# A four-level attention stack on one core: level 0's self attention as thirteen written steps, and level 2's steps reordered

## The chip, the cores and the metric

The kernel runs on one core of a Trainium2 chip. The metric is device time in microseconds (us) from launch to end; the median of three runs of the kernel before is 4409.24 us (4403.62 to 4411.94). The engines are named as the profile names them: PE (TensorE; its weight loads are PEld), DVE (VectorE), ACT (ScalarE), POOL (GpSimd) and SP (SyncE, which here only issues transfers).

## What is computed

A residual stream x of 64 sequences, 32 tokens and 256 features (2048 rows) goes through four levels of three layers: cross attention with a context, self attention, and a feed-forward layer, each on the layer norm of x and added to x. Two of the twelve layers matter here. Level 0's self attention has 16 heads of 16 features, with a root-mean-square norm of each head's query and key:

```python
def rms_norm(x, w):
    ms = jnp.mean(x * x, axis=-1, keepdims=True)
    return x * jax.lax.rsqrt(ms + EPS) * w
q = rms_norm(proj(Wq), qn_w)
k = rms_norm(proj(Wk), kn_w)
v = proj(Wv)
scores = jnp.einsum('bhnd,bhmd->bhnm', q, k) * scale
attn = jax.nn.softmax(scores, axis=-1)
out = jnp.einsum('bhnm,bhmd->bhnd', attn, v)
return out.transpose(0, 2, 1, 3).reshape(B, N, D) @ Wo.T
```

Level 2's self attention has 16 heads of 64 features, unit-length queries and keys, two constant extra keys a head, and a distance bias on the scores. Attention stays within one sequence of 32 tokens in both.

## The kernel before

The rows lie in 16 tiles of 128 rows (four sequences each), which stay in on-chip memory in self.x. Every layer is a loop over the 16 tiles (NT). All matrix work is float32 on PE; the results land in PSUM[...].

Level 0 self attention (`l0_attn`, L762 to L849) is a generator `body(i)` with four yields. `skewed` advances all live bodies once per round, oldest first, so five tiles are in flight: in one round tile i-4 makes its block diagonal of probabilities, its weighted sum of values and its output; i-3 its scores and softmax; i-2 its unit-length queries and keys (`qk`, L797, on POOL) and their transposes; i-1 its projections (queries and keys `pqk`, values `pv`), squares (L788) and mean squares (L792, L793) and the power -1/2 of these (`qk_r`, in `rsqrt`, L391 to L393, on POOL); tile i its layer norm (`layer_input`). Scores are 64 small matmuls (32 by 32 by 64); `kb` holds each key head pair twice, with one head of the pair zeroed by the weight kw, made by DVE at L804. `diagonal` (L872) is four DVE transposes of 32 by 512. PSUM is split into three banks "m" (projections, transposes, output), four for the scores "s", and one "o" for the weighted sum.

Level 2 self attention (`l2_attn`) has the same work as named steps, and a list written out by hand that says which step of which tile comes in which order within a round (i, i-1, i-2 and the next tile's norm i+1). `lengths(t, k)` sums the squares (L1928), bounds them (L1929) and takes the power on POOL (L1931), `unit` multiplies (L2041), `scores` ends with the maximum (L2083), the subtraction (L2084) and the exponential (L2085), `output` adds into x (L2120).

What sets the order on an engine: each engine runs its own stream in order and waits on semaphores. The streams are made by the tile framework, which schedules instructions as it believes that their operands and buffers become ready and takes the order in the program as a preference among those that are ready. So the streams need not follow the text, and in the trace they don't everywhere: in level 2 the maximum L2083 is written before the second half's multiply L2041, and runs behind it. All matmuls through the helper `mm` are recorded at L438, transposes at L432 (`transposed`) or L2151 (`transposed_into`).

Of the kernel before, what the change touches and what calls it, by code (L numbers as in the profile page):

```python
# [28 lines left out]
NB = 4  # L29
# [289 lines left out]
class Perceiver:  # L319
# [442 lines left out]
    def l0_attn(self):  # L762
# [3 lines left out]
        with ExitStack() as st:  # L766
            one = st.enter_context(tc.tile_pool(name="l0a_1", bufs=1))
            pool = st.enter_context(tc.tile_pool(name="l0a", bufs=3))
            ps = st.enter_context(tc.tile_pool(name="l0a_p", bufs=3, space=PSUM))
            bds = self.zeroed(one, [128, 16, NB, T], "bd")  # L770

            vs = self.zeroed(one, [128, 16, 32], "v", 4)
            qw = self.sb(one, [128, 1], "qw")
            nc.vector.tensor_scalar(qw, self.col("L0_attn_qn_w"), 0.25, None, ALU.mult)
            kw = self.sb(one, [128, 2], "kw")
            nc.vector.tensor_scalar(kw, self.table("pair"), self.col("L0_attn_kn_w"), None, ALU.mult)

            def body(i):
                _, nT = self.layer_input(pool, ps, i, "m")
                yield  # L780
                pqk = self.sb(ps, [128, 32, 16], "m")
                self.mm(pqk.rearrange("p h d -> p (h d)"), [(nT[:, k, :], wqkv[:, k, 0:512]) for k in range(2)])
                pv = self.sb(ps, [128, 16, 16], "m")
                self.mm(pv.rearrange("p h d -> p (h d)"), [(nT[:, k, :], wqkv[:, k, 512:768]) for k in range(2)])
                v = vs[i % 4]
                nc.scalar.copy(v[:, :, 0:16], pv)
                sq = self.sb(pool, [128, 32, 16], "sq")
                nc.scalar.activation(sq, pqk, AF.Square)  # L788
                raw = self.sb(pool, [128, 32, 16], "raw")
                nc.scalar.copy(raw, pqk)  # L790
                ms = self.sb(pool, [128, 32], "ms")
                nc.vector.tensor_reduce(ms, sq, AX.X, ALU.add)  # L792
                nc.vector.tensor_scalar(ms, ms, 1.0 / 16, None, ALU.mult)  # L793
                r = self.rsqrt(pool, ms, float(np.finfo(np.float32).eps), "qk_r")
                yield
                qk = self.sb(pool, [128, 32, 16], "qk")
                nc.gpsimd.tensor_tensor(qk, raw, bcast(r, 2, 16), ALU.mult)  # L797
                pT = self.transposed(ps, qk.rearrange("p h d -> p (h d)"), "m", 4)
                qT = self.sb(pool, [128, 2, 128], "qT")
                nc.scalar.activation(qT, pT[:, 0:2, :], AF.Copy, scale=qw)  # L800

                kb = self.sb(pool, [128, 2, NB, 2, T], "kb")
                for c in range(2):
                    nc.vector.tensor_tensor(  # L804
                        kb[:, c],
                        bcast(pT[:, 2 + c, :].rearrange("p (b t) -> p b t", b=NB), 2, 2),
                        bcast(bcast(kw, 1, NB), 3, T),
                        ALU.mult,
                    )
                yield  # L810

                psc = self.sb(ps, [128, 4, 512], "s", bufs=1)
                for c in range(2):
                    for r in range(4):
                        for b in range(NB):
                            q = slice(b * T, (b + 1) * T)
                            f = slice(32 * r, 32 * r + 32)
                            self.mm(
                                psc[q, r, c * 64 : c * 64 + 64],
                                [(qT[f, c, q], kb[f, c, b].rearrange("p h t -> p (h t)"))],  # L820
                            )
                sv = psc[:, :, 0:128].rearrange("p r (c h k) -> p c r h k", c=2, h=2)
                e = self.sb(pool, [128, 16, T], "hs_e")
                mx = self.sb(pool, [128, 16], "hs_m")
                for c in range(2):
                    ev = e[:, 8 * c : 8 * c + 8, :].rearrange("p (r h) k -> p r h k", r=4)
                    mv = mx[:, 8 * c : 8 * c + 8].rearrange("p (r h) -> p r h", r=4)
                    nc.vector.tensor_reduce(mv, sv[:, c], AX.X, ALU.max)
                    nc.vector.tensor_tensor(ev, sv[:, c], bcast(mv, 3, T), ALU.subtract)
                nc.scalar.activation(e, e, AF.Exp)  # L830
                rs = self.softmax_heads(pool, e, 16, T)
                p = self.sb(pool, [128, 16, T], "hs_p")
                nc.gpsimd.tensor_tensor(p, e, bcast(rs, 2, T), ALU.mult)
                yield
                bd = bds[i % 2]
                self.diagonal(bd, p)
                po = self.sb(ps, [128, 4, 128], "o", bufs=1)
                for h in range(16):
                    self.mm(
                        po[32 * (h % 4) : 32 * (h % 4) + 32, h // 4, :],  # L840
                        [(v[:, h, :], bd[:, h].rearrange("p b t -> p (b t)"))],
                    )
                oT = self.sb(pool, [128, 4, 128], "oT")
                nc.scalar.copy(oT, po)  # L844
                py = self.sb(ps, [128, D], "m")
                self.mm(py, [(oT[:, k, :], wo[:, k, :]) for k in range(4)])
                nc.vector.tensor_tensor(self.x[:, i, :], self.x[:, i, :], py, ALU.add)

            skewed(body(i) for i in range(NT))  # L849

    def heads_softmax(self, pool, src, bd, scale, plus=0.0):

# [1059 lines left out]
    def l2_attn(self):  # L1912
# [3 lines left out]
        with ExitStack() as st:  # L1916
# [148 lines left out]
            def scores(i):  # L2065
# [9 lines left out]
                for hh in range(2):  # L2075
# [3 lines left out]
                        bias.rearrange("p (c a) k -> p a c k", a=2)[:, hh],  # L2079
                        ALU.add,  # L2080
                    )
                mx = self.sb(pool, [128, 16], "mx")
                nc.vector.tensor_reduce(mx, s, AX.X, ALU.max)  # L2083
                nc.vector.tensor_tensor(s, s, bcast(mx, 2, K), ALU.subtract)  # L2084
                nc.scalar.activation(s, s, AF.Exp)  # L2085
                t_p[i] = s

            def divided(i):
                s = t_p[i]
# [33 lines left out]
            norm_1(0), norm_2(0), norm_3(0), turned(0)  # L2123
            for i in range(NT + 2):
                steps = [
                    (i, lambda t: projected(t, 0)),
                    (i, lambda t: lengths(t, 0)),
                    (i + 1, norm_1),
                    (i - 2, weighted),
                    (i, lambda t: projected(t, 1)),  # L2130
                    (i, lambda t: unit(t, 0)),
                    (i, lambda t: lengths(t, 1)),
                    (i + 1, norm_2),
                    (i - 1, scores),
                    (i - 2, output),
                    (i, lambda t: unit(t, 1)),
                    (i - 1, divided),
                    (i + 1, norm_3),
                    (i, value_rows),
                    (i, lambda t: heads_first(t, 0)),  # L2140
                    (i + 1, turned),
                    (i - 1, diagonal),
                    (i, lambda t: heads_first(t, 1)),
                ]
                for t, step in steps:
# [292 lines left out]
```

## Time and profile before

| | us |
|---|---|
| median of 3 runs | 4409.24 |
| profiled execution, own time | 4408.68 |
| its span, first to last instruction | 4406.9 |
| level 0 self attention, first square to last add into x | 399.12 to 632.07 |
| level 2 self attention, first square to last copy of a weighted sum | 2418.7 to 2820.6 |

| whole span | PE | PE weight loads | DVE | ACT | POOL |
|---|---|---|---|---|---|
| busy us | 3820.6 | 2664.1 | 1896.2 | 1177.4 | 1181.6 |
| share | 87% | 60% | 43% | 27% | 27% |

How to read the lines of the profile: `L792 DVE TENSOR_REDUCE ms<-sq 128x32 f32<-128x512 f32` is line 792 of the kernel, its engine, its operation, the tile written and the tiles read (buffer numbers left out) and their shapes. In a timeline the first number is the start in us from the start of the span, the second the duration, and a bracket gives how long the engine was idle before it and what released it. In a table of windows, "busy (x)" is an engine's busy time and number of instructions in that stretch, and PEclk is the TensorE clock that was granted, as a share of full speed. In a list of waits, the numbers are the total us, how many times, and the longest. A whole-span share is a mean over stages with different limits.

### The profile page before, as it was taken

How to read it: one execution, taken by the hardware profiler on the slowest of the kernel's cores; microseconds unless marked ns; L12 is line 12 of the kernel's file. 1: busy time of each engine (PE TensorE's matmuls, PEld its weight loads, DVE VectorE, ACT ScalarE, POOL GpSimd, SP SyncE). 2: the span in 40 equal slices, each digit the busy share in tenths (PEclk: the TensorE clock that was granted, in tenths of full speed). 3: DMA queues.
4: the chain of work that ended last, by engine and by line, in shares of the span. 5: the costliest groups of instructions: out<-in, count | busy, mean ns of one | idle time of the engine just before them, and what ended most of it. 6: DMA issues, size and time to landing. Idle time of an engine off the chain costs nothing.

```text
span 4406.9 us, 68988 instructions
## 1 busy us (share of the span) xinstructions
PE 3820.6 (87%) x27148; PEld 2664.1 (60%) x27148; DVE 1896.2 (43%) x5310; ACT 1177.4 (27%) x3159; POOL 1181.6 (27%) x1638
## 2 busy tenths in 40 slices
PE   7997662879898596989998888899999999999996
PEld 6785441556676364767675555444444677777774
DVE  5554654244444605565655555301000344444335
ACT  2342220123332022333332333201111233333331
POOL 5434641033311135444443333100000211112102
PEclk9998875989999698999999899999999999999997
DMA  6351021175000143222221000200001111110000
GB/s 213 123 160 37 1 108 65 42 234 166 3 2 28 55 124 109 73 71 69 79 73 51 1 1 1 81 0 0 0 0 38 37 33 33 33 33 21 2 2 22
DMA packets 162996, 245.25 MB, mean 56 GB/s; under 512 B 27521, under 2 KB 105745, under 8 KB 158449
## 3 DMA queue, kind: packets, MB, share of 16 engines
q1 hardware_dynamic: 152370, 224.92, 16.4%
q0 software_dynamic: 5280, 10.82, 1.1%
q10 hardware_dynamic: 5024, 5.11, 0.3%
q8 instruction: 215, 3.52, 0.3%
q14 instruction: 107, 0.88, 0.1%
HBM read 223.80 MB, written 16.99 MB: 55 GB/s over the span
## 4 chain that ended last, share of the span: by engine, by line
PE 43%; DVE 8%; POOL 6%; ACT 3%; issue 2%; DMA 1%; DVEq 0%; ACTq 0%; POOLq 0%; SPq 0%
PE m L438 20%; PE h L438 13%; PE s L438 4%; POOL sr L1931 2%; PE b L438 1%; PE e L2327 1%; ACT e L2314 1%; DVE t L2342 1%; POOL p L1874 1%; PE m L1880 1%; POOL cT L1835 1%; DVE qn L2041 1%; DVE ss L1928 1%; PE o L438 1%; PE m L432 1%
## 5 line engine op out<-in xcount | busy, mean ns | idle before, releaser
L438 PE MATMUL m<-w,oT 128*128 128x256 f32 x1344 | 336.9, 403 | 21.7 <-ACT oT L844 9.8
L438 PEld LDWEIGHTS m<-w,oT 128*128 128x128 f32 x1344 | 265.8, 201 | 78.5 <-ACT oT L844 14.0
L438 PE MATMUL m<-nTg,w 128*128 128x256 f32 x1024 | 231.3, 385 | 1.3 <-ACT nTg L1323 1.1
L438 PE MATMUL h<-h,w 128*128 128x512 f32 x512 | 220.4, 592 | 0.0
L438 PE MATMUL h<-h,h 128*128 128x512 f32 x512 | 220.4, 592 | 0.0
L2203 DVE TENSOR_TENSOR y<-m,row_L_ffn_w_s 128x256 f32<-128x256 f32 x16 | 6.8, 425 | 486.6 <-PE m L438 486.6
L438 PEld LDWEIGHTS m<-nTg,w 128*128 128x128 f32 x1024 | 193.5, 191 | 28.9 <-ACT nTg L1323 1.7
L2314 ACT ACTIVATE e<-s,nm 128x257 f32<-128x257 f32 x256 | 118.2, 474 | 321.6 <-DVE nm L2313 263.2
L438 PE MATMUL m<-w,nT 128*128 128x512 f32 (+2 forms) x384 | 173.9, 595 | 30.2 <-DVE x L2120 28.9
L438 PE MATMUL s<-cT,ut 128*128 128x257 f32 x768 | 186.0, 388 | 3.7 <-ACT p L1870 2.9
L438 PE MATMUL m<-pT,cn 128*128 128x384 f32 x512 | 177.3, 489 | 0.0
L1874 POOL TENSOR_TENSOR p<-p,rs 128x771 f32<-128x771 f32 x64 | 94.9, 1483 | 298.9 <-DVE rs L1873 260.7
L438 PEld LDWEIGHTS h<-h,w 128*128 128x128 f32 x512 | 97.3, 190 | 122.5 <-issue 122.5
L438 PEld LDWEIGHTS h<-h,h 128*128 128x128 f32 x512 | 97.3, 190 | 122.5 <-issue 122.5
L2204 POOL TENSOR_TENSOR x<-x,y 128x256 f32<-128x256 f32 x16 | 11.9, 744 | 591.8 <-DVE y L2203 591.8
L438 PEld LDWEIGHTS m<-v,eT 128*128 128x128 f32 x1280 | 158.5, 192 | 9.0 <-ACT qT L695 1.8
L872 DVE STREAM_TRANSPOSE bd<-hs_p 32x512 f32<-32x512 f32 x192 | 134.9, 702 | 59.5 <-POOL hs_p L866 38.7
L438 PEld LDWEIGHTS s<-cT,ut 128*128 128x128 f32 x768 | 143.9, 195 | 27.0 <-issue 4.2
L438 PE MATMUL m<-v,eT 128*128 128x64 f32 x1280 | 158.4, 271 | 1.4 <-DVE eT L2331 0.7
L2196 ACT ACTIVATE h<-h,cols 128x512 f32<-128x512 f32 x64 | 44.0, 687 | 397.1 <-PE h L438 397.1
L438 PEld LDWEIGHTS m<-w,nT 128*128 128x128 f32 x384 | 79.2, 214 | 99.2 <-DVE x L2120 40.5
L438 PEld LDWEIGHTS m<-pT,cn 128*128 128x128 f32 x512 | 94.8, 190 | 58.5 <-issue 2.4
(612 smaller groups left out, 8120.5 us busy)
## 6 DMA issues: line engine op xcount, KB each, us to landing
ct<-in_ctx SPq DMA_DIRECT2D x192, 256.0 KB
cT<-in_ctxT SPq DMA_DIRECT2D x32, 1028.0 KB
cT<-in_ctxT SPq DMA_DIRECT2D x128, 257.0 KB
ab<-abd SPq DMA_DIRECT2D x64, 257.0 KB
rb<-rd SPq DMA_DIRECT2D x16, 514.0 KB
w_all<-in_l0f_w SPq DMA_DIRECT2D x8, 1024.0 KB
w<-in_l1f_down SPq DMA_DIRECT2D x8, 640.0 KB
extra<-maskd SPq DMA_DIRECT2D x16, 257.0 KB
```

The source lines that it names most:

```text
L432: self.nc.tensor.transpose(out[:, c, :], src[:, c * 128 : (c + 1) * 128], self.ident)
L438: self.nc.tensor.matmul(out, lhsT=l, rhs=r, start=j == 0, stop=j == last)
L872: self.nc.vector.transpose(bd[q, :, b, :], p[q])
L1835: nc.gpsimd.tensor_tensor(cT, cT, bcast(ab[:, 0, :], 1, 2), ALU.mult)
L1874: nc.gpsimd.tensor_tensor(p, p, bcast(rs, 2, S), ALU.mult)
L1880: nc.tensor.transpose(pp[:, g, :], p[:, g, c * 128 : (c + 1) * 128], self.ident)
L1928: nc.vector.tensor_reduce(ss, sq, AX.X, ALU.add)
L1931: nc.gpsimd.tensor_tensor(r, ss, self.neg_half[:p].to_broadcast([p, nh]), ALU.pow)
L2041: nc.vector.tensor_tensor(t, pq, bcast(r, 2, 64), ALU.mult)
L2314: nc.scalar.activation(e[:, r, :], pss[r], AF.Exp, bias=nm[:, r : r + 1], accum_out=ss[:, r : r + 1])
L2327: nc.tensor.transpose(pe[:, r, :], e[:, r, c * 128 : (c + 1) * 128], self.ident)
L2342: nc.vector.tensor_tensor(t[q], t[q], po[q, :, j, :], ALU.add)
```

## The change

Level 0: the generator becomes thirteen named steps over tiles i+1 (norm), i (projection and powers), i-1 (unit length, transposes and key forms), i-2 (scores, softmax, diagonal) and i-3 (weighted sum, output), run in a written list. Within the steps:

- the power of the 32 mean squares is taken in two instructions of 16 columns each (`lengths`), at two places of the list; epsilon is added in the DVE instruction that scales the mean squares
- the copy `raw` of the queries and keys goes; `unit` on DVE multiplies them straight from PSUM, instead of POOL from `raw`
- the key forms `kb` are made by two ACT instructions in place of two on DVE
- maximum and subtraction of the scores take one instruction each in place of two
- PSUM is divided anew: one bank "m" in place of three, two banks for queries and keys "qk", four "s" and one "o", which the output now shares

Level 2: `exponentials` becomes a step of its own, and the list is in another order. Each tile's arithmetic is as before.

```diff
--- before.py
+++ after.py
@@ -766,7 +766,7 @@
         with ExitStack() as st:
             one = st.enter_context(tc.tile_pool(name="l0a_1", bufs=1))
             pool = st.enter_context(tc.tile_pool(name="l0a", bufs=3))
-            ps = st.enter_context(tc.tile_pool(name="l0a_p", bufs=3, space=PSUM))
+            ps = st.enter_context(tc.tile_pool(name="l0a_p", bufs=1, space=PSUM))
             bds = self.zeroed(one, [128, 16, NB, T], "bd")
 
             vs = self.zeroed(one, [128, 16, 32], "v", 4)
@@ -774,42 +774,74 @@
             nc.vector.tensor_scalar(qw, self.col("L0_attn_qn_w"), 0.25, None, ALU.mult)
             kw = self.sb(one, [128, 2], "kw")
             nc.vector.tensor_scalar(kw, self.table("pair"), self.col("L0_attn_kn_w"), None, ALU.mult)
-
-            def body(i):
-                _, nT = self.layer_input(pool, ps, i, "m")
-                yield
-                pqk = self.sb(ps, [128, 32, 16], "m")
-                self.mm(pqk.rearrange("p h d -> p (h d)"), [(nT[:, k, :], wqkv[:, k, 0:512]) for k in range(2)])
+            t_n, t_nT, t_qk, t_r, t_T, t_e, t_o = ({} for _ in range(7))
+
+            def norm_1(i):
+                st = self.sb(pool, [128, 6], "ln_st")
+                nc.vector.bn_stats(st, self.x[:, i, :])
+                mv = self.sb(pool, [128, 2], "ln_mv")
+                nc.vector.bn_aggr(mv, st)
+                t_n[i] = mv, self.rsqrt(pool, mv[:, 1:2], LN_EPS, "ln_r")
+
+            def norm_2(i):
+                mv, r = t_n[i]
+                n = self.sb(pool, [128, D], "n")
+                nc.vector.tensor_scalar(n, self.x[:, i, :], mv[:, 0:1], r, ALU.subtract, ALU.mult)
+                t_n[i] = n
+
+            def turned(i):
+                pt = self.sb(ps, [128, 2, 128], "m")
+                self.transposed_into(pt, t_n[i], 2)
+                nT = self.sb(pool, [128, 2, 128], "nT")
+                nc.scalar.copy(nT, pt)
+                t_nT[i] = nT
+
+            def projected(i):
+                nT, v = t_nT[i], vs[i % 4]
                 pv = self.sb(ps, [128, 16, 16], "m")
                 self.mm(pv.rearrange("p h d -> p (h d)"), [(nT[:, k, :], wqkv[:, k, 512:768]) for k in range(2)])
-                v = vs[i % 4]
                 nc.scalar.copy(v[:, :, 0:16], pv)
+                pqk = self.sb(ps, [128, 32, 16], "qk", bufs=2)
+                self.mm(pqk.rearrange("p h d -> p (h d)"), [(nT[:, k, :], wqkv[:, k, 0:512]) for k in range(2)])
                 sq = self.sb(pool, [128, 32, 16], "sq")
                 nc.scalar.activation(sq, pqk, AF.Square)
-                raw = self.sb(pool, [128, 32, 16], "raw")
-                nc.scalar.copy(raw, pqk)
                 ms = self.sb(pool, [128, 32], "ms")
                 nc.vector.tensor_reduce(ms, sq, AX.X, ALU.add)
-                nc.vector.tensor_scalar(ms, ms, 1.0 / 16, None, ALU.mult)
-                r = self.rsqrt(pool, ms, float(np.finfo(np.float32).eps), "qk_r")
-                yield
+                nc.vector.tensor_scalar(
+                    ms, ms, 1.0 / 16, float(np.finfo(np.float32).eps), ALU.mult, ALU.add
+                )
+                t_qk[i] = pqk
+                t_r[i] = ms, self.sb(pool, [128, 32], "qk_r")
+
+            def lengths(i, half):
+                ms, r = t_r[i]
+                f = slice(16 * half, 16 * half + 16)
+                nc.gpsimd.tensor_tensor(r[:, f], ms[:, f], self.neg_half.to_broadcast([128, 16]), ALU.pow)
+
+            def unit(i):
                 qk = self.sb(pool, [128, 32, 16], "qk")
-                nc.gpsimd.tensor_tensor(qk, raw, bcast(r, 2, 16), ALU.mult)
-                pT = self.transposed(ps, qk.rearrange("p h d -> p (h d)"), "m", 4)
+                nc.vector.tensor_tensor(qk, t_qk[i], bcast(t_r[i][1], 2, 16), ALU.mult)
+                t_qk[i] = qk.rearrange("p h d -> p (h d)")
+
+            def heads_first(i):
+                pT = self.transposed_into(self.sb(ps, [128, 4, 128], "m"), t_qk[i], 4)
                 qT = self.sb(pool, [128, 2, 128], "qT")
                 nc.scalar.activation(qT, pT[:, 0:2, :], AF.Copy, scale=qw)
 
                 kb = self.sb(pool, [128, 2, NB, 2, T], "kb")
-                for c in range(2):
-                    nc.vector.tensor_tensor(
-                        kb[:, c],
-                        bcast(pT[:, 2 + c, :].rearrange("p (b t) -> p b t", b=NB), 2, 2),
-                        bcast(bcast(kw, 1, NB), 3, T),
-                        ALU.mult,
-                    )
-                yield
-
-                psc = self.sb(ps, [128, 4, 512], "s", bufs=1)
+                for hh in range(2):
+                    nc.scalar.activation(
+                        kb[:, :, :, hh, :],
+                        pT[:, 2:4, :].rearrange("p c (b t) -> p c b t", b=NB),
+                        AF.Copy,
+                        scale=kw[:, hh : hh + 1],
+                    )
+                t_T[i] = qT, kb
+
+            def scores(i):
+                qT, kb = t_T[i]
+
+                psc = self.sb(ps, [128, 4, 512], "s")
                 for c in range(2):
                     for r in range(4):
                         for b in range(NB):
@@ -819,34 +851,66 @@
                                 psc[q, r, c * 64 : c * 64 + 64],
                                 [(qT[f, c, q], kb[f, c, b].rearrange("p h t -> p (h t)"))],
                             )
-                sv = psc[:, :, 0:128].rearrange("p r (c h k) -> p c r h k", c=2, h=2)
+                sv = psc[:, :, 0:128].rearrange("p r (x k) -> p r x k", x=4)
+
                 e = self.sb(pool, [128, 16, T], "hs_e")
                 mx = self.sb(pool, [128, 16], "hs_m")
-                for c in range(2):
-                    ev = e[:, 8 * c : 8 * c + 8, :].rearrange("p (r h) k -> p r h k", r=4)
-                    mv = mx[:, 8 * c : 8 * c + 8].rearrange("p (r h) -> p r h", r=4)
-                    nc.vector.tensor_reduce(mv, sv[:, c], AX.X, ALU.max)
-                    nc.vector.tensor_tensor(ev, sv[:, c], bcast(mv, 3, T), ALU.subtract)
+                mv = mx.rearrange("p (r x) -> p r x", r=4)
+                nc.vector.tensor_reduce(mv, sv, AX.X, ALU.max)
+                nc.vector.tensor_tensor(
+                    e.rearrange("p (r x) k -> p r x k", r=4), sv, bcast(mv, 3, T), ALU.subtract
+                )
                 nc.scalar.activation(e, e, AF.Exp)
+                t_e[i] = e
+
+            def divided(i):
+                e = t_e[i]
                 rs = self.softmax_heads(pool, e, 16, T)
                 p = self.sb(pool, [128, 16, T], "hs_p")
                 nc.gpsimd.tensor_tensor(p, e, bcast(rs, 2, T), ALU.mult)
-                yield
-                bd = bds[i % 2]
-                self.diagonal(bd, p)
-                po = self.sb(ps, [128, 4, 128], "o", bufs=1)
+                t_e[i] = p
+
+            def diagonal(i):
+                self.diagonal(bds[i % 2], t_e[i])
+
+            def weighted(i):
+                v, bd = vs[i % 4], bds[i % 2]
+                po = self.sb(ps, [128, 4, 128], "o")
                 for h in range(16):
+                    c, r, hh = h // 8, (h // 2) % 4, h % 2
                     self.mm(
                         po[32 * (h % 4) : 32 * (h % 4) + 32, h // 4, :],
-                        [(v[:, h, :], bd[:, h].rearrange("p b t -> p (b t)"))],
+                        [(v[:, h, :], bd[:, 4 * r + 2 * c + hh].rearrange("p b t -> p (b t)"))],
                     )
                 oT = self.sb(pool, [128, 4, 128], "oT")
                 nc.scalar.copy(oT, po)
-                py = self.sb(ps, [128, D], "m")
-                self.mm(py, [(oT[:, k, :], wo[:, k, :]) for k in range(4)])
+                t_o[i] = oT
+
+            def output(i):
+                py = self.sb(ps, [128, D], "o")
+                self.mm(py, [(t_o[i][:, k, :], wo[:, k, :]) for k in range(4)])
                 nc.vector.tensor_tensor(self.x[:, i, :], self.x[:, i, :], py, ALU.add)
 
-            skewed(body(i) for i in range(NT))
+            norm_1(0), norm_2(0), turned(0)
+            for i in range(NT + 3):
+                steps = [
+                    (i, projected),
+                    (i + 1, norm_1),
+                    (i - 1, unit),
+                    (i, lambda t: lengths(t, 0)),
+                    (i - 1, heads_first),
+                    (i - 2, scores),
+                    (i + 1, norm_2),
+                    (i - 3, weighted),
+                    (i + 1, turned),
+                    (i - 2, divided),
+                    (i, lambda t: lengths(t, 1)),
+                    (i - 3, output),
+                    (i - 2, diagonal),
+                ]
+                for t, step in steps:
+                    if 0 <= t < NT and not (t == 0 and step in (norm_1, norm_2, turned)):
+                        step(t)
 
     def heads_softmax(self, pool, src, bd, scale, plus=0.0):
 
@@ -2079,11 +2143,14 @@
                         bias.rearrange("p (c a) k -> p a c k", a=2)[:, hh],
                         ALU.add,
                     )
+                t_p[i] = s
+
+            def exponentials(i):
+                s = t_p[i]
                 mx = self.sb(pool, [128, 16], "mx")
                 nc.vector.tensor_reduce(mx, s, AX.X, ALU.max)
                 nc.vector.tensor_tensor(s, s, bcast(mx, 2, K), ALU.subtract)
                 nc.scalar.activation(s, s, AF.Exp)
-                t_p[i] = s
 
             def divided(i):
                 s = t_p[i]
@@ -2123,23 +2190,24 @@
             norm_1(0), norm_2(0), norm_3(0), turned(0)
             for i in range(NT + 2):
                 steps = [
+                    (i - 2, diagonal),
                     (i, lambda t: projected(t, 0)),
+                    (i + 1, norm_1),
                     (i, lambda t: lengths(t, 0)),
-                    (i + 1, norm_1),
                     (i - 2, weighted),
+                    (i + 1, norm_2),
                     (i, lambda t: projected(t, 1)),
                     (i, lambda t: unit(t, 0)),
+                    (i + 1, norm_3),
+                    (i - 1, scores),
                     (i, lambda t: lengths(t, 1)),
-                    (i + 1, norm_2),
-                    (i - 1, scores),
+                    (i - 1, exponentials),
                     (i - 2, output),
                     (i, lambda t: unit(t, 1)),
                     (i - 1, divided),
-                    (i + 1, norm_3),
                     (i, value_rows),
                     (i, lambda t: heads_first(t, 0)),
                     (i + 1, turned),
-                    (i - 1, diagonal),
                     (i, lambda t: heads_first(t, 1)),
                 ]
                 for t, step in steps:
```

## The prediction

> **What bounds the kernel now.** I read the page first: TensorE (PE) is busy for 87% of the span, but that is a mean over twelve stages, so I looked at the two stages that the diff touches. The view of windows gives each from its first projection to its end:
>
> ```profile
> core 0: us, PE busy (x) PEld busy (x) DVE busy (x) ACT busy (x) POOL busy (x), PEclk, DMA share, GB/s
> 399.00:632.00 233.00, 148.76 (x1883) 98.43 (x1881) 124.84 (x280) 53.10 (x111) 137.70 (x98) 0.80 0.02 6
> 2418.00:2825.00 407.00, 352.07 (x3556) 218.33 (x3554) 205.54 (x365) 128.30 (x189) 129.70 (x99) 0.95 0.03 9
> ```
>
> In level 0's 233 us no engine is full: PE 64%, POOL 59%, DVE 54%, and PE's granted clock is only 0.80. Something circulates. In level 2's 407 us PE is 87% busy at 0.95, so at most an eighth is to be had. DMA is idle in both, and the change moves no DMA.
>
> What circulates in level 0 is seen in the timeline of POOL alone (start, duration, instruction; brackets: idle before):
>
> ```profile
> 504.01 1.06 POOL L797 TENSOR_TENSOR qk<-raw,qk_r 128x512 f32<-128x512 f32 x1
> 505.03 0.23 POOL L391 TENSOR_SCALAR ln_r_v<-ln_mv 128x1 f32<-128x1 f32 x1
> 505.34 0.57 POOL L393 TENSOR_TENSOR ln_r<-ln_r_v,neg_half 128x1 f32<-128x1 f32 x1
> 507.56 1.05 POOL L833 TENSOR_TENSOR hs_p<-hs_e,sh_r 128x512 f32<-128x512 f32 x1 [1.66 <-DVE sh_r L516]
> 511.50 0.31 POOL L391 TENSOR_SCALAR qk_r_v<-ms 128x32 f32<-128x32 f32 x1 [2.89 <-DVE ms L793]
> 511.90 5.46 POOL L393 TENSOR_TENSOR qk_r<-qk_r_v,neg_half 128x32 f32<-128x32 f32 x1
> 517.43 1.06 POOL L797 TENSOR_TENSOR qk<-raw,qk_r 128x512 f32<-128x512 f32 x1
> ```
>
> The same multiply comes back after 13.42 us. In between, by the timelines of the other engines: PE waits for it and transposes (505.12 to 506.03), and only behind these transposes, in its own order, projects the next tile (to 509.15); ScalarE (ACT) squares, DVE sums and scales (to 511.41, one 0.70 us diagonal piece in between), POOL adds epsilon and takes the power, and multiplies again. So 1.11 multiply + 0.91 transposes + 3.12 projection + 0.63 square + 1.72 mean square + 0.40 + 5.53 power = 13.42. The level-0 squares run from 399.12 to 599.53, 15 rounds of 13.36. The view of waits agrees:
>
> ```profile
> POOL qk_r_v L391 <- DVE ms L793: 62.0, 15, 7.2
> PEld m L432 <- POOL qk L797: 48.1, 15, 9.6
> ```
>
> Level 2 repeats every 24.65 us (DVE's timeline, one round's second half):
>
> ```profile
> 2591.67 1.22 DVE L1928 TENSOR_REDUCE ss<-sq 128x16 f32<-128x1024 f32 x1
> 2592.80 0.43 DVE L2076 TENSOR_TENSOR s<-c,con 128x272 f32<-128x272 f32 x1
> 2593.14 0.17 DVE L1929 TENSOR_SCALAR ss<-ss 128x16 f32<-128x16 f32 x1
> 2593.22 0.43 DVE L2076 TENSOR_TENSOR s<-c,con 128x272 f32<-128x272 f32 x1
> 2596.33 1.23 DVE L2041 TENSOR_TENSOR qn<-b,sr 128x1024 f32<-128x1024 f32 x1 [2.67 <-POOL sr L1931]
> 2597.47 0.71 DVE L2083 TENSOR_REDUCE mx<-s 128x16 f32<-128x544 f32 x1
> 2598.21 0.72 DVE L2084 TENSOR_TENSOR s<-s,mx 128x544 f32<-128x544 f32 x1
> 2598.86 0.41 DVE L2120 TENSOR_TENSOR x<-x,m 128x256 f32<-128x256 f32 x1
> ```
>
> The maximum is ready at 2593.65 but stands behind qn, which waits for a power. The text writes the maximum before qn; the stream has it behind. So the written order is a preference of the scheduler, not the issue order, and I can't read the new streams off the diff. Behind this come exponential, sum, quotient, diagonal and, on PE, `weighted`, the two projections, the next square and power: that loop is the 24.65, of which PE idles 2.07 (for x) and 1.46 (for the diagonal).
>
> **Level 0, part by part.** Per tile:
> - POOL loses the multiply (1.06) and the epsilon add (0.34, now folded into DVE's scaling at no cost: the same instruction with a second operand). The power becomes two of 16 columns. Level 2 has just that shape: sr<-ss,neg_half, 128x16, 2.906 us. Two are 5.81 against 5.45. POOL: 8.7 before, 5.81 + 1.05 (quotient) + 0.79 (layer norm) = 7.65 after.
> - DVE loses the two key forms (2 x 0.395) and gains `unit`, 128x512 out of PSUM. The nearest row is the subtraction L862 hs_e<-s of level 3, the same shape out of PSUM: 0.69. Two maxima and two subtractions (4 x 0.42) become one each at that row's 0.69. DVE: 8.5 before, 8.1 after.
> - ACT loses `raw` (0.58) and gains two key forms of 128x256, at qT's row 0.474 each: about 4.0 a tile. It has room; but the forms hold the only "m" bank for about 1.5 us, then `turned` needs it. Scores and `weighted` (0.85 + 1.1 on PE) stand between and cover that; without them it would cost 1.5 a round.
> - PE's work is unchanged: transposes 0.5, projection 2.83, turning 0.34, scores 0.8, weighted 1.1, output 2.65 = 8.2 at full clock (the rounds at 505 and 519 show the same steps slow and fast; slow they make 10.6).
> - Moved: the projection of tile i now stands before the transposes of tile i-1. Nothing in it waits for the power of its neighbour, so the 13.4 loop is cut. New wait: PE's transposes stand behind `unit` on DVE, behind both halves on POOL; scores, `weighted` and the next projection queue behind them on PE.
>
> What is late next? Power to power now takes two rounds. In the unfavourable but, after level 2's stream, likely issue order both halves run ahead of the quotient, and `unit` ahead of the softmax sum: powers 5.81, unit 0.79, sum and reciprocal 0.94, quotient 1.15, diagonal 2.85, weighted 1.1, copy of oT 0.7, output 2.65, projection 2.83, square to scaled mean 1.8: 20.6 for two rounds, 10.3 each at full clock. In the favourable order (quotient between the halves) the powers, unit and PE's round make about 18.2, 9.1 each; engine floors are PE 8.2 and DVE 8.1. In the bad one (`unit` between maximum and subtraction, subtraction and exponential then joining the loop, +1.3 for the two rounds) it is 10.9.
>
> The clock decides the rest. Row: 0.80 over this stage, though its repeated PE gaps are only 2.0 to 2.3 us; level 2 with gaps of 2.1 and 1.5 has 0.95. [...] By the row, PE's 8.2 becomes 10.3 and with the wait for oT 11.0. Shorter gaps should lie between; I take **10.5**, ends 9.2 and 11.6. Gain: 15 x (13.36 - 10.5) = 43.
>
> Tail: from the last square (599.53) to the last x (632.07) it is 32.5 now, in rounds of 13. Afterwards only tile 15's chain is left: square and mean 1.7, powers 5.8 with a quotient between 1.1, unit 0.8, transposes 0.6, forms 1.55, scores 0.85, maximum and subtraction 1.4, exponential 0.7, sum 1.0, quotient 1.15, diagonal 2.9, weighted 1.3, copy 0.7, output 3.4, x 0.4 = 25.4; with 2 for tiles 13 and 14, 27.5: gain 5. Level 0 in all **-48** (-26 to -68).
>
> **Level 2.** No instruction is added or removed. `diagonal` at the end of a round or at the head of the next has only PE and ACT work between: nothing on DVE changes. The norm steps move earlier into idle DVE time (the trace already has them early), cover: about 3 us of DVE idle before ss; uncovered, about 1.4 us a round. What counts is `scores` before the second `lengths` and the exponentials as a step of their own behind it. The scaled ss then stands behind both s additions: the power starts about 0.4 us later. If mx alone slips ahead of qn, subtraction and exponential start about 0.3 earlier: -4 over 15 rounds. If nothing passes qn: +6. If mx and subtraction both pass it, the exponential comes 3.4 us earlier and PE's two gaps (3.5) close down to its 21.1 busy: -40. I take -4, as the scheduler let qn pass a dependent pair before.
>
> **Sum.** The profiled execution took 4408.68 (span 4406.9), 0.56 under the median 4409.24. 4409 - 48 - 4 = **4357**.
>
> **Rivals**
> - Likeliest (0.55): as above, 4335 to 4380.
> - Smaller (0.18): the clock stays at 0.8, rounds of 11.6, no tail gain, level 2 +6: 4409 - 26 + 6 = 4389. For it: DVE at 8.1 and PE at 10.6 would both be nearly full, each stalling the other in order.
> - Larger (0.14): level 2's loop is cut too: rounds of 10.0, 4409 - 55 - 40 = 4314. For it: DVE is idle just when mx could run; against it: the present stream.
> - Slower (0.08): the scheduler, which placed qn ahead of mx, pulls a tile's `unit` and transposes ahead of the next projection on PE. Then the loop is back inside one round with a single "m" bank: powers 5.81, quotient 1.1, unit 0.8, transposes 0.9, forms holding the bank 1.6, projection 3.7, square and mean 1.7 = 15.6: +34, 4443. It decides once that sum exceeds 13.36. Against it: the projection is ready earlier and is written first.
> - Not doing what it says (0.05): the stream keeps the old rotation and its 13.4: about 4405.
>
> Within 0.2% (8.8 us, about what a measurement of this kernel tells from no change) lie the last case and a bit of the second: 0.07; slower 0.08; faster 0.85. The range 4315 to 4400 leaves out half of the larger case and the last two, 0.2.
>
> **What would show it.** Right: level-0 squares 10 to 11 us apart; two powers of 2.9 a tile; PE's projection issued without a wait for POOL; PE's largest waits there for the diagonal or `unit`, under 2 us a round; stage clock above 0.85; level 2 still near 24.4 a round with qn before the subtraction. Wrong: squares 13 us apart or more, transposes before the projection in PE's order, waits for "m" behind ACT's forms, or a level-2 round below 23 or above 25.

## The result and the profile after

The changed kernel takes 4417.21 us (median of 17 runs, 4407.97 to 4424.51), the kernel before 4408.69 beside it (17 runs): a ratio of 1.0018 with a 95% interval of 1.0011 to 1.0026, so about 8 us slower. The profiled execution of after took 4410.83 (span 4409.1), only 2 us more than the one of before. That is less than the medians differ by; the last section names a stall that is in the one profile and not in the other. 4357 was predicted.

The windows of the two stages, in after:

```profile
core 0: us, PE busy (x) PEld busy (x) DVE busy (x) ACT busy (x) POOL busy (x), PEclk, DMA share, GB/s
391.00:637.00 246.00, 158.79 (x1879) 104.79 (x1878) 118.50 (x231) 56.85 (x127) 122.63 (x84) 0.72 0.02 5
2424.00:2820.00 396.00, 336.38 (x3543) 208.13 (x3542) 204.79 (x363) 128.99 (x189) 129.69 (x98) 0.97 0.03 9
```

Level 0 now stretches over 246 us, DVE and POOL have less to do than before (118.5 and 122.6 us busy, against 133.8 and 143.1 in the same window of before), and the granted clock is 0.72. Its squares start at 391.29, 395.99, 409.12 and so on up to 591.52: 200.2 us from the first to the last, where before has 200.4. The last eight (487.25 to 591.52) are 104.27 / 7 = 14.9 apart, where before's last eight are 12.9 apart; over all 15 rounds the mean is 13.35 in after and 13.36 in before, because after's first rounds are shorter. From the start of the last square to the end of the last add into x it takes 45.9 (591.52 to 637.42), where before has 32.5.

One late round in DVE's timeline of after, from one mean square to the next:

```profile
493.61 0.67 DVE L809 TENSOR_REDUCE ms<-sq 128x32 f32<-128x512 f32 x1
494.32 0.18 DVE L810 TENSOR_SCALAR ms<-ms 128x32 f32<-128x32 f32 x1
500.37 0.69 DVE L823 TENSOR_TENSOR qk<-qk,qk_r 128x512 f32<-128x512 f32 x1 [5.87 <-POOL qk_r L819]
500.98 0.68 DVE L859 TENSOR_REDUCE hs_m<-s 128x16 f32<-128x512 f32 x1
501.69 0.69 DVE L860 TENSOR_TENSOR hs_e<-s,hs_m 128x512 f32<-128x512 f32 x1
...
503.14 0.69 DVE L512 TENSOR_REDUCE sh_s<-hs_e 128x16 f32<-128x512 f32 x1 [0.22 <-ACT hs_e L863]
503.86 0.25 DVE L516 RECIPROCAL sh_r<-sh_s 128x16 f32<-128x16 f32 x1
...
505.34 2.85 DVE L936 STREAM_TRANSPOSE bd<-hs_p 32x512 f32<-32x512 f32 x4 [0.95 <-POOL hs_p L870]
508.22 0.43 DVE L419 BATCH_NORM_STATS2 ln_st<-x 128x6 f32<-128x256 f32 x1
508.57 0.67 DVE L809 TENSOR_REDUCE ms<-sq 128x32 f32<-128x512 f32 x1
```

The same stretch of POOL:

```profile
494.58 5.76 POOL L819 TENSOR_TENSOR qk_r<-ms,neg_half 128x16 f32<-128x16 f32 x2 [4.22 <-DVE ms L810]
503.01 0.22 POOL L391 TENSOR_SCALAR ln_r_v<-ln_mv 128x1 f32<-128x1 f32 x1 [2.67 <-DVE ln_mv L783]
503.31 0.58 POOL L393 TENSOR_TENSOR ln_r<-ln_r_v,neg_half 128x1 f32<-128x1 f32 x1
504.26 1.05 POOL L870 TENSOR_TENSOR hs_p<-hs_e,sh_r 128x512 f32<-128x512 f32 x1 [0.37 <-DVE sh_r L516]
509.53 5.76 POOL L819 TENSOR_TENSOR qk_r<-ms,neg_half 128x16 f32<-128x16 f32 x2 [4.22 <-DVE ms L810]
```

Read the two together. The text has `unit` of tile i-1 on DVE behind the mean square of the next tile i. In the stream of after, `unit` stands right behind the mean square of its own tile and waits 5.87 us until POOL has done both halves of that tile's power, which run one after the other ("x2") although the text puts the quotient between them. The maximum, the subtraction, the sum and the diagonals of older tiles, none of which needs these powers, queue behind `unit` on DVE, and their exponential (ACT) and quotient (POOL) come between them. The next tile's square is done at 503.86 (start 503.26, 0.60 long, in ACT's timeline), but its mean square stands behind the diagonals until 508.57, 4.7 us later. So everything is in one round again, now through DVE's order instead of PE's. Start to start: mean square .97, powers 5.79, `unit` .61, maximum .71, subtraction and exponential 1.45, sum .72, reciprocal .40, quotient 1.08, diagonals and a layer-norm statistic 3.23: 14.96, the round.

The list of waits of after says the same in three of its lines:

```profile
DVE qk L823 <- POOL qk_r L819: 84.8, 15, 6.4
ACT hs_e L863 <- DVE hs_e L860: 53.5, 10, 6.2
PE o L438 <- DVE bd L936: 47.5, 15, 4.4
```

The first is the wait itself, 5.7 us in each of 15 rounds. The other two, the exponential waiting for the subtraction and PE for the diagonals, stand behind `unit` in DVE's order, so I read them as that same wait passed on. PE's timeline shows that the projection does run ahead of the transposes, with no wait for POOL:

```profile
499.56 1.25 PE L438 MATMUL m<-w,nT 128*128 128x256 f32 x4
500.64 1.88 PE L438 MATMUL qk<-w,nT 128*128 128x512 f32 x4
503.42 0.66 PE L2219 MATMUL m<-ident,qk 128*128 128x128 f32 x4 [0.90 <-ACT v L803]
```

Level 2, in DVE's timeline of after:

```profile
2572.62 0.16 DVE L1993 TENSOR_SCALAR ss<-ss 128x16 f32<-128x16 f32 x1
2572.74 0.72 DVE L2151 TENSOR_REDUCE mx<-s 128x16 f32<-128x544 f32 x1
2575.80 1.23 DVE L2105 TENSOR_TENSOR qn<-b,sr 128x1024 f32<-128x1024 f32 x1 [2.34 <-POOL sr L1995]
2576.94 0.72 DVE L2152 TENSOR_TENSOR s<-s,mx 128x544 f32<-128x544 f32 x1
```

The maximum has slipped ahead of the second half's qn, the subtraction has not. A round is 24.23 us (24.65 before), and first square to last copy of a weighted sum is 394.8 (2424.5 to 2819.3) against 401.9.

### The profile page after: what moved, and what is told of

Its sections match the earlier page's. It is cut to its first block, busy times and chain, and to the rows that moved or that the text cites. A ratio compares the mean times of both kernels' runs of the same rounds, so it can differ in the third digit from the quotient of the medians.

```text
span 4409.1 us, 68941 instructions
## 1 busy us (share of the span) xinstructions
PE 3824.0 (87%) x27148; PEld 2666.7 (60%) x27148; DVE 1883.8 (43%) x5262; ACT 1180.9 (27%) x3175; POOL 1165.2 (26%) x1622
## 4 chain that ended last, share of the span: by engine, by line
PE 43%; DVE 8%; POOL 6%; ACT 3%; issue 2%; DMA 1%; DVEq 0%; ACTq 0%; POOLq 0%
PE m L438 20%; PE h L438 13%; PE s L438 4%; POOL sr L1995 2%; PE b L438 1%; PE e L2395 1%; ACT e L2382 1%; DVE t L2410 1%; PE m L1944 1%; DVE bd L936 1%; POOL cT L1899 1%; DVE qn L2105 1%; DVE ss L1992 1%; POOL p L1938 1%; DMA cT<-in_ctxT 1%
## 5 line engine op out<-in xcount | busy, mean ns | idle before, releaser
L438 PE MATMUL m<-w,oT 128*128 128x256 f32 x1216 | 293.7, 394 | 11.9 <-DVE oT L1447 4.0
L438 PEld LDWEIGHTS m<-w,oT 128*128 128x128 f32 x1216 | 235.8, 197 | 59.6 <-DVE oT L2340 10.8
L438 PE MATMUL m<-w,nT 128*128 128x512 f32 (+2 forms) x320 | 132.6, 548 | 26.6 <-DVE x L2187 23.2
L438 PE MATMUL o<-bd,v 128*64 128x128 f32 (+1 forms) x1536 | 96.3, 327 | 58.6 <-DVE bd L936 58.6
L1995 POOL TENSOR_TENSOR sr<-ss,neg_half 128x16 f32<-128x16 f32 (+1 forms) x33 | 93.5, 2833 | 140.1 <-DVE ss L1993 140.1
```

Source lines behind the costliest of these rows:

```text
L438: self.nc.tensor.matmul(out, lhsT=l, rhs=r, start=j == 0, stop=j == last)
L1995: nc.gpsimd.tensor_tensor(r, ss, self.neg_half[:p].to_broadcast([p, nh]), ALU.pow)
```

## The experiments

The theory after the result: level 0's time is set by the order in which DVE and POOL issue, not by the work in it. The rivals: the single "m" bank, or the clock.

**Each half alone.** The kernel before with the diff's part for `l0_attn` alone, and with its part for `l2_attn` alone.

> Only level 0's self attention is changed. Theory (a chain on DVE: unit waits for both powers in front of the softmax, and the next mean square stands behind the diagonals): stage as in the changed kernel, last add into x about 5 us later than before, ratio 1.001 to 1.003. Rival (the two stages' changes disturb each other through prefetch): a ratio away from that of the whole change less level 2's gain.

> Only level 2's order is changed. Theory: rounds of 24.2 in place of 24.65, 6 to 7 us less in the stage, ratio about 0.9985. Rival (level 2 carries the loss of the whole change): ratio above 1.001.

Level 0 alone: 4427.99, ratio 1.0029 (1.0018 to 1.0041). Level 2 alone: 4408.0, ratio 0.9983 (0.9976 to 0.999). Against 4415.31 of before on their chip that is +12.7 and -7.3, and their sum, +5.4, lies in the interval of the whole change (+5 to +11). The profiles agree: from the last weighted-sum copy of the layer before (L749) to level 0's last add it takes 248.0 in before and 260.6 with level 0's change alone, 242.5 with level 2's alone and 255.0 in after. The first two profiles have the stall that the last section tells of, the other two have not; in either pair level 0's change costs 12.5.

**DVE bound to the written order.** In after, for level 0: a dependency of issue order only, without a semaphore, from each instruction of an engine to the one before it in the program:

```
+            at = len(nc.cur_bb.bb.instructions)
             norm_1(0), norm_2(0), turned(0)
...
+            self.chained(at, (mybir.EngineType.DVE,))
...
+    def chained(self, start, engines):
...
+                self.tc.add_manual_dep(
+                    rows[k],
+                    last[e],
+                    mybir.DependencyInfo(mybir.DependencyClass.NoSync, mybir.DependencyReason.DATA),
...
```

> The changed kernel, with DVE's level-0 instructions bound to the written order (order of issue only, no added waits on data). The mean square and unit stand where the text has them. Theory (DVE's issue order sets the rounds): level-0 rounds of 11 to 12 us in place of 14.7, time about 40 to 50 us below the changed kernel. Rival (the single PSUM bank m and the bank shared by weighted sum and output set the rounds, or PE's clock): rounds stay above 13.5, time within 15 us of the changed kernel.

Measured: 4430.56, ratio 1.0037 (1.0024 to 1.005), rounds of 14.8 as the mean of all 15, against 13.35 in after. My theory in that form failed: `unit` waits for nothing any more, and nothing is gained. POOL's timeline of this kernel has the reason:

```profile
500.17 5.76 POOL L819 TENSOR_TENSOR qk_r<-ms,neg_half 128x16 f32<-128x16 f32 x2 [5.82 <-DVE ms L810]
505.90 0.22 POOL L391 TENSOR_SCALAR ln_r_v<-ln_mv 128x1 f32<-128x1 f32 x1
506.20 0.56 POOL L393 TENSOR_TENSOR ln_r<-ln_r_v,neg_half 128x1 f32<-128x1 f32 x1
```

and its DVE, one line further:

```profile
506.80 0.41 DVE L789 TENSOR_SCALAR n<-x,ln_mv,ln_r 128x256 f32<-128x256 f32 x1 [4.27 <-POOL ln_r L393]
507.13 0.68 DVE L512 TENSOR_REDUCE sh_s<-hs_e 128x16 f32<-128x512 f32 x1
```

The text has the next tile's norm on POOL before the halves. POOL issues it behind both, so the normed tile waits for 5.76 us of powers, and with it the softmax sum on DVE, and on PE its transposes and the next projection. The loop has only changed engines.

**The power taken out of the time.** In after:

```
-                nc.gpsimd.tensor_tensor(r[:, f], ms[:, f], self.neg_half.to_broadcast([128, 16]), ALU.pow)
+                nc.gpsimd.tensor_tensor(r[:, f], ms[:, f], self.neg_half.to_broadcast([128, 16]), ALU.mult)
```

> The changed kernel with the two powers of each tile replaced by a multiply of the same shape, so that the queries and keys are not brought to unit length: this leaves out that part of the computation. Theory (the wait of unit for the powers is a link of the round's chain): rounds fall by nearly the powers' 5 us, to about 10. Rival (PSUM banks): rounds stay above 12.5.

4342.84, ratio 0.9836 (0.9818 to 0.9854). The late rounds have the same order on DVE as after's; this is one of them, from mean square to `unit`, on DVE and POOL:

```profile
507.10 0.69 DVE L809 TENSOR_REDUCE ms<-sq 128x32 f32<-128x512 f32 x1
508.14 0.39 POOL L819 TENSOR_TENSOR qk_r<-ms,neg_half 128x16 f32<-128x16 f32 x2 [3.96 <-DVE ms L810]
508.57 0.69 DVE L823 TENSOR_TENSOR qk<-qk,qk_r 128x512 f32<-128x512 f32 x1 [0.57 <-PE m L2219]
```

(The last bracket names PE, but POOL's pair ended at 508.53, just before `unit` starts.) Both halves take 0.39 us in place of 5.76. The last eight squares are 9.2 apart in place of 14.9, the mean of all rounds is 8.35 in place of 13.35. The late round lost 5.7 with 5.4 of power, so the power is inside the loop with its whole length, and PE and the banks allow late rounds of 9.2.

**The banks.** "m" gets two and "qk" one, of the same eight.

```
-                pv = self.sb(ps, [128, 16, 16], "m")
+                pv = self.sb(ps, [128, 16, 16], "m", bufs=2)
...
-                pqk = self.sb(ps, [128, 32, 16], "qk", bufs=2)
+                pqk = self.sb(ps, [128, 32, 16], "qk")
```

> The changed kernel with two PSUM banks m and one bank for queries and keys, in place of one and two. Theory (order behind the powers): rounds stay at 14 to 15. Rival (the single bank m sets the rounds): rounds fall to 12.5 or less.

4430.62, ratio 1.0037 (1.0028 to 1.0045), late rounds of 14.65, as after's last five (14.62 to 14.69). The "m" bank is not what holds these rounds. What it would cost in shorter rounds isn't shown, and this run also takes a bank from "qk".

**DVE and POOL bound.** As above with both engines in the list.

> As the run with DVE bound to the written order, and POOL bound to it too, so that the layer norm's power and the softmax quotient no longer stand behind both halves of the long power. Theory (the rounds are set by what stands behind the powers in an engine's order, and binding DVE alone only moved the wait from unit to the next tile's norm): rounds of 11 to 12, about 40 us below the changed kernel. Rival (the new PSUM division or PE itself holds 14 us rounds): no better than 13.5.

4362.12, ratio 0.9876 (0.9846 to 0.9907), rounds of 10.14, where I had expected 11 to 12. Then the same with `unit` at the head of the list:

```
+                    (i - 1, unit),
                     (i, projected),
                     (i + 1, norm_1),
-                    (i - 1, unit),
```

> As with DVE and POOL bound to the written order, with unit moved to the head of the list, so that PE's transposes find it done behind the projection. Theory: rounds of about 10 (9.5 to 10.8), 55 to 70 us below the changed kernel. Rival (PSUM banks or PE's order): above 12.

4366.31, ratio 0.9887 (0.9862 to 0.9911), rounds of 10.12: no difference clear of the intervals. Between these two places, the place of `unit` decides nothing: it waits for its powers in no round of the first run and in two of the second.

**POOL alone bound.**

> The changed kernel with only POOL bound to the written order in level 0: norm power, first half, quotient, second half. DVE's order is left to the scheduler, which can then no longer believe unit to be ready before the softmax sum, since the quotient stands ahead of the second half. Theory (what stood behind the powers is what cost): rounds of 10 to 11, within 10 us of the run with both bound. Rival (DVE must be bound too): rounds above 13.

4343.07, ratio 0.9861 (0.9841 to 0.9881), rounds of 9.12: shorter than I had expected (10 to 11), and 63 us below before where both bound gave 50. Its POOL:

```profile
493.15 0.22 POOL L391 TENSOR_SCALAR ln_r_v<-ln_mv 128x1 f32<-128x1 f32 x1
493.45 0.57 POOL L393 TENSOR_TENSOR ln_r<-ln_r_v,neg_half 128x1 f32<-128x1 f32 x1
495.01 2.90 POOL L819 TENSOR_TENSOR qk_r<-ms,neg_half 128x16 f32<-128x16 f32 x1 [0.98 <-DVE ms L810]
498.36 1.05 POOL L870 TENSOR_TENSOR hs_p<-hs_e,sh_r 128x512 f32<-128x512 f32 x1 [0.44 <-DVE sh_r L516]
499.36 2.89 POOL L819 TENSOR_TENSOR qk_r<-ms,neg_half 128x16 f32<-128x16 f32 x1
```

and its DVE around the same tile's `unit`:

```profile
499.44 2.85 DVE L938 STREAM_TRANSPOSE bd<-hs_p 32x512 f32<-32x512 f32 x4
502.32 0.69 DVE L823 TENSOR_TENSOR qk<-qk,qk_r 128x512 f32<-128x512 f32 x1
502.93 0.68 DVE L809 TENSOR_REDUCE ms<-sq 128x32 f32<-128x512 f32 x1
```

Norm, half, quotient, half: the quotient leaves after 2.9 us of power, the diagonals run while POOL takes the second half, and `unit` finds its powers ready, without a bracket. The edit binds POOL only, but the scheduler's order for DVE changed with it: `unit` now stands behind the diagonals. The window from 440 to 530 in before, after and this run (the clock is the third number from the end):

```profile
440.00:530.00 90.00, 62.07 (x822) 40.70 (x820) 54.40 (x126) 23.13 (x48) 59.06 (x44) 0.86 0.01 1
440.00:530.00 90.00, 61.07 (x728) 41.49 (x721) 44.92 (x94) 22.07 (x49) 51.51 (x36) 0.76 0.00 1
440.00:530.00 90.00, 75.70 (x1124) 50.01 (x1123) 70.98 (x138) 33.95 (x76) 73.38 (x50) 0.98 0.01 3
```
That the DVE-bound version has 10.14 and not 9.12 can be read off DVE: in strict order it is busy or waits out its own softmax (1.18 for the exponential, 0.95 for the quotient) all round long, 8.0 + 2.1; left free it puts other instructions there.

**Level 2's other order.** Before's level 0; level 2 in the new order with DVE bound, and `divided` of tile i-1 ahead of the second `unit`:

```
+                    (i - 1, divided),
                     (i, lambda t: unit(t, 1)),
-                    (i - 1, divided),
...
+            self.chained(at, (mybir.EngineType.DVE,))
```

> Only level 2 changed, with its DVE instructions bound to the written order and the softmax quotient written before the second unit: maximum, subtraction and sum all pass the multiply that waits for the power. Theory (the power is in level 2's loop only because the softmax stands behind that multiply): rounds of 21.3 to 22.5, close to PE's 21.1 busy, ratio 0.988 to 0.993. Rival (level 2 is bound by PE with its weight loads and small gaps): rounds stay above 23.7, ratio 0.997 or more.

4361.24, ratio 0.9878 (0.9848 to 0.9908). A round is 21.33, PE's busy time in it 20.8. DVE's timeline of this kernel:

```profile
2575.73 0.71 DVE L2087 TENSOR_REDUCE mx<-s 128x16 f32<-128x544 f32 x1
2576.48 0.73 DVE L2088 TENSOR_TENSOR s<-s,mx 128x544 f32<-128x544 f32 x1
2577.19 0.42 DVE L2123 TENSOR_TENSOR x<-x,m 128x256 f32<-128x256 f32 x1
2577.99 0.72 DVE L512 TENSOR_REDUCE sh_s<-s 128x16 f32<-128x544 f32 x1 [0.37 <-ACT s L2089]
2578.74 0.25 DVE L516 RECIPROCAL sh_r<-sh_s 128x16 f32<-128x16 f32 x1
2579.03 0.19 DVE L2097 TENSOR_TENSOR p<-s,sh_r 128x32 f32<-128x32 f32 x1
2579.14 1.22 DVE L2041 TENSOR_TENSOR qn<-b,sr 128x1024 f32<-128x1024 f32 x1
```

The maximum, the subtraction, the sum and the quotient run in the time for which the second half's qn would have stood waiting for its power, and this qn then waits for nothing. It is what the prediction's "larger" case describes: -40 there, though its own gaps of 3.5 us over 15 rounds make 53, and -51 was measured. Which of the two edits does it, the moved quotient or the bound order, isn't separated.

**All together.** First with DVE and POOL bound in level 0, then with POOL alone.

> Level 0 changed with DVE and POOL bound to the written order, and level 2 in the changed order with DVE bound to it and the quotient ahead of the second unit. Theory (two separate loops, each cut in its own stage): the gains add, ratio 0.975 to 0.980, about 4310. Rival (the gains overlap, or the clock takes part back): ratio above 0.983.

> Level 0 with POOL alone bound to the written order (the quicker of the level 0 versions), and level 2 as in the run with DVE bound and the quotient ahead of the second unit. Theory (two separate loops, each held by its own engine's order): the gains add, 66 + 47 = about 113 us, so about 4296 us, ratio 0.972 to 0.978. Rival (the two gains overlap, or the shorter level 0 costs clock in what follows): above 0.981, that is no better than the pair with DVE and POOL bound.

4316.24, ratio 0.9795 (0.9778 to 0.9811), and 4300.97, ratio 0.975 (0.9733 to 0.9766). The gains of the two loops add: with POOL bound alone it was 63, of which 7 are level 2's own, so 56 for level 0; with 51 for level 2 that is 107, and 109 (4409.67 to 4300.97) were measured. This is the fastest version of the study. It is the change itself, with one step of level 2 moved and the written order enforced on one engine in each stage.

## Why the prediction was wrong

What failed is one step of the level 0 part: "Power to power now takes two rounds." I saw that cutting the projection loose from the transposes breaks the old loop on PE, and it does (projection before transposes, no wait for POOL). I then closed the new loop through PE (diagonal, weighted, output, projection, square) over two rounds, and never asked where the next mean square stands on DVE. It stands behind the diagonals, so the whole softmax, the diagonals and the powers are in one round: 14.9 instead of 20.6 / 2. Of the issue order I had even the bad case named, `unit` between maximum and subtraction; in the last eight rounds of the trace it is a place earlier, ahead of the maximum. But I charged it 1.3 us over two rounds, where it puts the maximum, the subtraction and all behind them after 5.8 us of power in each round. The run without the power shows that this is the loop: the late rounds fall from 14.9 to 9.2.

- The rounds: -43 predicted. From the first square to the last, 0 measured (200.2 against 200.4): the late rounds are 2 us longer than before's, and the first ones shorter.
- The tail: -5 predicted, +13 measured. In after, with no projection left to do, the last three weighted sums start 9.1 and 9.8 us apart (611.92, 621.03, 630.78 on PE), each behind its own chain of maximum, subtraction, exponential, sum, quotient and diagonals on DVE, where a tile's maximum is issued behind the older tile's diagonals. I had credited the last tile with a chain that meets no other. Rounds and tail together make about the +12.5 that level 0's change costs.
- The clock: above 0.85 predicted, 0.72 granted. PE now stops for 3.4 to 4.4 us for the diagonals in late rounds, and the clock is lower than the 0.80 of before. From 440 to 530 it is 0.76 in after, and 0.98 with POOL bound and nothing else edited. The cause thus runs the other way from my rival "the clock stays at 0.8": the clock followed the order of issue. How it follows isn't shown. In the same window it is 0.92 in the run without the power, which has no PE gap over 1.7 us from 490 to 512, and 0.85 in the run with DVE bound, which has gaps of 4.85 and 4.09 from 490 to 520, against at most 4.37 in after. I also read before's gaps as 2.0 to 2.3: in its window from 440 to 530, at 0.86, there are smaller ones and two of 3.5 and 3.6. So the longest gap alone doesn't give the clock, and what does stays open. My 10.5 lay between 10.3 at full clock and 11.0 at the clock of before; that these rounds could come to full clock was my estimate, the stage in before had 0.80.
- The slower rival: near the late rounds in its sum (15.6 predicted, 14.9 measured), but by luck, since the sum is of other terms. It had the transposes ahead of the projection on PE and the "m" bank held; neither is in the trace, and two "m" banks leave the late rounds as they were. What it had right is that the scheduler could pull `unit` forward. I gave it 0.08 because I asked only what could bring the loop back into one round on PE.
- Right: the two halves (5.81 predicted, 5.76 measured), `unit` 0.69, maximum 0.68, key forms (2 x 0.474 predicted, 0.83 for both), epsilon in DVE's scaling at no cost (0.18, in before without it as in after with it), DMA still near idle (0.02 in the stage).
- Luck: the 10.14 with DVE and POOL bound and the 9.12 with POOL bound lie near my 10.3 and 9.1, but not for my reasons. In the first, DVE's own order sets the round and no power is waited for. In the second, `unit` follows its own tile's mean square within one round (493.85 to 502.32), not two. And the terms that I named for the favourable order (powers 5.81, `unit` 0.79, PE's round 8.2) make 14.8 of the 18.2; the rest isn't written down.
- Level 2: right in its mechanism (the maximum alone slips ahead of qn), -4 predicted and -7 measured.

What stays open as well: why the framework issues both halves ahead of the quotient and of the next norm. The trace shows the order and the runs show its price, not the scheduler's reason.

## What to carry over

A loop has to be closed through every engine that it touches: after cutting it on PE, ask for each other engine which instruction of the next tile stands behind which instruction of the older ones (in after, the maximum behind a `unit` that waited 5.87 us). The long instructions here (5.76 us of power on POOL) did their harm through what was queued behind them and behind their reader. Which engine has to keep a written order has to be tried: in level 0 binding POOL was worth some 72 us (63 below before, where after is 8.5 above) and binding DVE alone nothing; in level 2 DVE was bound, with one step moved, and that gave 51. If the streams are made by a scheduler, price the order that it is likely to issue, and bind the order before judging a reordering.

## What the runs showed of the hardware

At the head of level 0 POOL clears the block diagonals and value tiles while DVE makes two layer norms. In before, DVE:

```profile
387.67 5.99 DVE L425 TENSOR_SCALAR n<-x,ln_mv,ln_r 128x256 f32<-128x256 f32 x2 [0.68 <-POOL ln_r L393]
```

and POOL beside it:

```profile
388.10 3.55 POOL L504 MEMSET bd<- 128x2048 f32 x2
391.58 1.93 POOL L504 MEMSET v<- 128x512 f32 x4
```

The same two instructions take 0.93 us in after, where DVE starts them at 386.07 and the memsets begin at 386.99, after them; in before they ended together with the memsets (393.66 and 393.51). It is the second of the pair that stalled: it began at 388.18, just behind the start of the first memset (388.10), and took 5.47 us, where one alone takes 0.41. The stall comes and goes from one profile to the next, whichever kernel it is: level 0's change alone has it (5.47 for the second norm, and 16.0 us from the last weighted-sum copy of the layer before to the first square, 15.1 in before), level 2's alone hasn't (9.8 for the same stretch, 8.8 in after). POOL's memsets run beside it; what holds the norm isn't shown. The stall may be why the profile of after lies 6 us under its median, and so nearer to before's than the medians are; that is argued, not shown. Before with the clearing put on DVE:

```
-            self.nc.gpsimd.memset(t, 0.0)
+            (eng or self.nc.gpsimd).memset(t, 0.0)
...
-            bds = self.zeroed(one, [128, 16, NB, T], "bd")
+            bds = self.zeroed(one, [128, 16, NB, T], "bd", eng=nc.vector)
-            vs = self.zeroed(one, [128, 16, 32], "v", 4)
+            vs = self.zeroed(one, [128, 16, 32], "v", 4, eng=nc.vector)
```

> The kernel before, with level 0's zeroing of the diagonal and value buffers (POOL memsets, 5.5 us) done on DVE in place of POOL. Theory (the two layer norms of 5.99 us at 387.67 stood blocked beside POOL's memsets, and the changed kernel's earlier start comes from its issuing them before the memsets, not from the new steps): the two norms take under 1.2 us, the first square comes 5 to 7 us earlier, ratio 0.9985 to 1.0. Rival (the norms wait for something else): the norms stay near 6 us.

4409.47, ratio 1.0005 (0.9994 to 1.0016). The norms took 0.93 and the first square came 8 us after the layer before instead of 15, but the memsets on DVE (two of 1.76 and the small ones) hold up the first mean squares, and the time is the same within the interval. The stall is seen; a gain from taking it away is not.
